# A graph network in two layers: TensorE's waits and semaphore raises gathered to one of each a chunk, and the sums of scores moved by one chunk

## The chip, the cores and the metric

The kernel runs on one core of one Trainium2 chip. A core has five engines that run their own instruction streams [...]: TensorE (PE in the profile, its weight loads PEld), VectorE (DVE), ScalarE (ACT), GpSimd (POOL) and SyncE (SP). An instruction that another one has to wait for raises its engine's semaphore when it ends; the one that waits does so until the semaphore has reached a given value. In this kernel SP issues the plain transfers between the chip's memory (HBM) and the core's own memory, and POOL issues the indirect ones, which gather or scatter single rows by a list of indices. The metric is the device time of one execution in microseconds, the median of the runs shown.

## What is computed

A graph of 10,000 nodes with 64 features each and 160,000 edges goes through two graph layers. The first is a softmax aggregation with four rounds, the second an attention without a division. Cut to what matters here:

```python
def genconv(x, src, dst, ea, ..., t):              # four rounds, l = 0..3
    m = relu(x[src] + ea) + EPS                    # one row for each edge
    logits = m * t
    mx = segment_max(logits, dst)
    e = exp(logits - mx[dst])
    denom = segment_sum(e, dst)
    agg = segment_sum(m * e / denom[dst], dst)
    h = (agg + x) @ W1 + b1
    return relu(layernorm(h)) @ W2 + b2

def attention(x, edge_attr, src, dst):             # once
    score = K[src] * Q[dst] / sqrt(8) * (edge_attr @ WE + bE)   # 8 heads of 8
    score = exp(clip(score.sum(over each head), -5, 5))
    return segment_sum(V[src] * score, dst)
```

The edges come sorted by dst, so every segment sum or maximum can be made as a scan along the edges with a mark where a new node begins.

## The kernel before

**Tiling.** The edge list is cut in two halves that lie on partitions 0 to 63 and 64 to 127, features down the partitions, edges along the free axis; the second half is walked backwards. A group is 128 edges of each half, a chunk four groups (512 columns). There are 625 groups and 158 chunks: 155 full ones, then two of two groups and one of one.

**A softmax layer** (`softmax_layer`, called four times, its layers are called 0 to 3 here). For chunk k, `front` has POOL gather eight blocks of 128 rows of the node table, one for each group and half (L738 through `gather`, L650), into a buffer `xg`, of which there are seven. TensorE then makes z: first the edge features times eencW (L740, one matmul over the whole chunk), then for each group the gathered rows, turned through the identity (L742), added on the same bank. The banks for z go round in five: z three times, then ept, then hist (`z_bank`; in layer 0 three of z alone). ScalarE takes z through a relu and the temperature (L745, L746) to `lg`, VectorE makes the running maximum (L752) and the difference (L754), ScalarE the exponentials (L757 to L767). `back`, for the chunk before, has VectorE make e*m (L780), two decaying scans (L782, L785), and two transposes (L811), and SP stores the result with four transfers (L815). SP also loads for each chunk, three chunks ahead, the marks (two transfers, L709) and the edge features (`load_ea`, L660, four buffers). Layer 0 has the edge features in rows: SP loads `er` (L667, L669), TensorE turns them (L678, L679), ScalarE copies them (L682) and SP stores them for the later layers (L683). Layer 0 also counts the nodes' edges as it goes: VectorE makes 0/1 matrices (`count`, L420, L423), TensorE multiplies them (`add_counts`, L429).

**Node layers.** Between two softmax layers `node_layer` gathers the sums of each node (POOL, `n_g`), runs the small matrices and writes the next table.

**The attention layer** (`attention_layer`). For each chunk SP loads the queries (L1045), the marks and the edge features; POOL gathers rows of keys and values (eight gathers again, into `kv`, a tile for two groups, seven tiles). `ahead` turns the queries on TensorE (L1055, bank oe), multiplies the edge features (L1058, bank hist), and VectorE spreads the queries by a scan (L1060) and multiplies (L1064, `eq`). `scores` turns keys (pk) and values (pv) on TensorE (L1084, three banks z in rotation), VectorE multiplies pk into eq (L1087), TensorE sums over each head (head_sum, L1089, bank dec). `weights` clips (VectorE, L1095) and takes the exponential (ScalarE, L1096). `back`, for the chunk before, multiplies pv by the weights (L1103), scans (L1105), transposes (L1116); SP stores with four transfers (L1120). At the end POOL gathers each node's row (`n_h`) and SP writes the output.

**Order.** The kernel is written in a language whose framework works out which instruction waits for which, from the buffers that they write and read, and sets the semaphores. An engine's instructions run in the order in which they stand in its stream; `InOrder` fixes that order to the order of the program text inside a layer. An instruction gets a semaphore raise when some wait counts on it: in the softmax layers before, all five matmuls of a chunk do, since each gather of chunk k+7 waits for the matmul that reads its own part of the buffer. Each matmul of L742 waits for its own two gathers.

Of the kernel before, what the change touches and what calls it, by code (L numbers as in the profile page):

```python
# [16 lines left out]
P = 128  # L17
# [9 lines left out]
def kernel(ctx: ExitStack, tc: tile.TileContext, a, out):  # L27
# [398 lines left out]

    def add_counts(ph, ol, oh, j0, j1):
        for k in range(j1 - j0):
            nc.tensor.matmul(ph, ol[:, k, :], oh[:, k, :], start=(j0 + k == 0),  # L429
                             stop=(j0 + k == R * KT - 1))  # L430

    def place_nodes(pool, cnt, tag):

# [213 lines left out]
    nc.vector.memset(zeros, 0.0)  # L647

    def gather(t, table, idx):
        nc.gpsimd.indirect_dma_start(out=t, out_offset=None, in_=table,  # L650
                                     in_offset=bass.IndirectOffsetOnAxis(ap=idx, axis=0))

    def span(k):
        g0, n = chunks[k]
# [2 lines left out]
    def load_ea(k):  # L657
        g0, n, cols = span(k)
        ea = edge.tile([P, CE], F32, name="ea", bufs=4)
        nc.sync.dma_start(ea[:, :n * G], eaT[:, cols])  # L660
        return ea

    def load_rows(k, ea_rows):
# [47 lines left out]

    V, S = nc.vector, nc.scalar

    def softmax_layer(l, ea_rows=None):

        prev = {}
        ph = ps("hist", [P, NT]) if ea_rows is not None else None
        per = 9
        if ph is not None:
# [12 lines left out]
        def front(k, marks, ea):  # L732
            g0, n, cols = span(k)
            m = n * G
            xg = edge.tile([P, CG, 2, D], F32, name="xg", bufs=7)
            for g in range(n):
                for s in range(2):
                    gather(xg[:, g, s, :], tables[l], index(g0 + g, s))  # L738
            z = z_bank(k)
            nc.tensor.matmul(z[:, :m], eencW, ea[:, :m], start=True, stop=False)  # L740
            for g in range(n):
                nc.tensor.matmul(z[:, g * G:(g + 1) * G], xg[:, g, :, :].rearrange("p s d -> p (s d)"),  # L742
                                 ident, start=False, stop=(g == n - 1))
            lg = ps("lg", [P, CE])
            S.activation(lg[:, :m], z[:, :m], AF.Relu)  # L745
# [80 lines left out]
        for k in range(NC):  # L826
            if k + lead < NC:
                got.append(fetch(k + lead))
            z, u, up, e = front(k, got[k][0], eas[k])
            if k + 2 < NC:  # L830
                eas.append(columns_of(k + 2))
            for c in counts:
                add_counts(*c)
            if counts and counts[-1][-1] == R * KT:
                rows_of_nodes(edge, ph)
            if held is not None:
                back(k - 1, *held)
            held = z, u, decay(k, up), e
            counts = history(k)
            order()  # L840
# [197 lines left out]
    def attention_layer():  # L1038

        prev = {}  # L1040

        def fetch(k):
            g0, n, cols = span(k)
            q = edge.tile([P, CG, 2, D], F32, name="q", tag="er", bufs=3)
            nc.sync.dma_start(  # L1045
                q[:, :n], qs[2 * g0 * G:2 * (g0 + n) * G, :].rearrange("(g p s) d -> p g s d", p=G, s=2))
            return load_marks(k, keeps_d), q, load_ea(k)

        def ahead(k, keep, q, ea):

# [7 lines left out]
            nc.tensor.matmul(pe[:, :m], WE, ea[:, :m], start=True, stop=True)  # L1058
            qh = edge.tile([P, CE], F32, name="qh", tag="u")
            V.tensor_tensor_scan(qh[:, :m], keep[:, :m], pq[:, :m], prev.get("q", zero1),  # L1060
                                 op0=OP.mult, op1=OP.add)
            prev["q"] = qh[:, m - 1:m]
            eq = edge.tile([P, CE], F32, name="eq", tag="sm")
            V.scalar_tensor_tensor(eq[:, :m], pe[:, :m], bE, qh[:, :m], op0=OP.add, op1=OP.mult)  # L1064
            return eq

        def fetch_kv(k):
            g0, n, cols = span(k)
            kvs = []
            for g in range(n):  # L1070
                if g % 2 == 0:
                    kvs.append(edge.tile([P, 2, 2, D2], F32, name="kv", tag="xg", bufs=7))
                for s in range(2):
                    gather(kvs[-1][:, g % 2, s, :], kv_table, index(g0 + g, s))
            return kvs

        def scores(k, kvs, eq):
            g0, n, cols = span(k)
            m = n * G
            pk = ps_a([P, CE])  # L1080
            pv = ps_a([P, CE])
            for pt, d0 in ((pk, 0), (pv, 1)):
                for g in range(n):
                    nc.tensor.matmul(pt[:, g * G:(g + 1) * G],  # L1084
                                     kvs[g // 2][:, g % 2].rearrange("p s d -> p (s d)")[:, d0::2],
                                     ident, start=True, stop=True)
            V.tensor_mul(eq[:, :m], pk[:, :m], eq[:, :m])  # L1087
# [123 lines left out]
```

## Time and profile before

| | |
|---|---|
| median of 3 runs | 10301.92 us (10288.25 to 10304.86) |
| the profiled execution's own time | 10286.74 us |
| its span in the trace | 10285.0 us |
| mean granted TensorE clock | 0.634 of full speed |
| gathers of softmax layer 0, from first start to last end | 159.5 to 1992.6 us |
| of layer 1 | 2223.1 to 3999.4 us |
| of layer 2 | 4217.1 to 5992.1 us |
| of layer 3 | 6210.4 to 7984.2 us |
| of the attention layer | 8338.0 to 10147.8 us |
| from a softmax layer's last gather to the next stage's first, layers 1 to 3 | 53.5 us |

The last six rows are read from the timeline of POOL. In a row of the costliest groups, the line and the engine come first, then the operation, what it writes and reads, how often, its busy time in us and the mean of one in ns, and after the second bar the idle time of the engine just before these instructions, with what ended most of it. "issue" is idle time for which the trace shows no wait; "remote" means that the trace doesn't tell who raised the semaphore that was waited for. In a timeline row, the start and the length in us come first, and the brackets hold the idle time before it. In a list of waits, a row gives the us in total, how many there were, and the longest. SP's rows have a q because they are its queue's own.

### The profile page before, as it was taken

What the parts mean: (1) busy time and instruction counts of PE and PEld (TensorE: products, weight loads), DVE (VectorE), ACT (ScalarE), POOL (GpSimd) and SP (SyncE); (2) the same over time, 40 slices, a digit from 0 to 9 for tenths busy, and PEclk for the clock granted to TensorE, in tenths of its full rate; (3) what the DMA queues carried; (4) which work ended last, traced back from release to release, by engine and by line L of the source; (5) the groups of instructions that cost most, each with busy time, mean ns of one, the idle gap of its engine ahead of it and who ended that gap; (6) DMA issues with size and microseconds to landing.
All of it is one profiled execution on the core that took longest, in us unless ns stands there. A gap on an engine that the chain in (4) does not pass through costs nothing. (4 is left out here: it accounts for less than half of the span.)

```text
span 10285.0 us, 67533 instructions
## 1 busy us (share of the span) xinstructions
PE 4024.4 (39%) x15722; PEld 2683.3 (26%) x15722; DVE 5480.7 (53%) x7537; ACT 2795.4 (27%) x4787; POOL 6369.3 (62%) x6736
## 2 busy tenths in 40 slices
PE   3444444452333333433333343333333444444442
PEld 1333333321222221222222222222222233333332
DVE  3767677625555554355555543555555445555553
ACT  1333333332333333333333332333333310000000
POOL 2666666556666665566666645666666456666665
PEclk8666666665655555655555565555556667777776
DMA  3555555654444444244444433444444235555553
GB/s 108 124 121 126 121 123 125 136 156 93 104 103 103 106 104 98 53 104 105 103 104 105 104 85 67 104 105 102 105 105 104 65 89 124 122 124 127 125 125 86
DMA packets 2467718, 1103.63 MB, mean 107 GB/s; under 512 B 2047265, under 2 KB 2239911, under 8 KB 2467088
## 3 DMA queue, kind: packets, MB, share of 16 engines
q1 hardware_dynamic: 2252120, 827.12, 34.1%
q0 software_dynamic: 215200, 272.11, 12.5%
q8 instruction: 140, 2.29, 0.1%
q14 instruction: 258, 2.11, 0.1%
HBM read 626.48 MB, written 471.91 MB: 107 GB/s over the span
## 5 line engine op out<-in xcount | busy, mean ns | idle before, releaser
L650 POOL DMA_INDIRECT xg<-table,idxA x2500 | 2364.9, 946 | 1939.4 <-remote 830.6
L650 POOL DMA_INDIRECT xg<-table,idxB x2500 | 2364.6, 946 | 763.1 <-issue 761.5
L752 DVE TENSOR_TENSOR_SCAN u<-lg,u,marks 128x512 f32<-128x512 f32 (+1 forms) x628 | 798.4, 1271 | 2712.9 <-ACT lg L746 1861.0
L740 PE MATMUL z<-ea,eencW 128*128 128x512 f32 (+1 forms) x892 | 872.0, 1079 | 2109.6 <-DMA marks<-ends_d 852.5
L742 PEld LDWEIGHTS z<-ident,xg 128*128 128x128 f32 x3512 | 802.6, 312 | 599.3 <-issue 572.4
L650 POOL DMA_INDIRECT kv<-kv_table,idxA x625 | 591.2, 946 | 434.6 <-remote 219.8
L742 PE MATMUL z<-ident,xg 128*128 128x128 f32 x3512 | 795.7, 396 | 157.6 <-DMA xg<-table,idxB 87.5
L740 PEld LDWEIGHTS z<-ea,eencW 128*128 128x128 f32 x892 | 226.7, 312 | 2191.5 <-issue 1907.2
L782 DVE TENSOR_TENSOR_SCAN se<-dec,se,e 128x512 f32<-128x512 f32 (+1 forms) x628 | 792.2, 1261 | 0.0
L785 DVE TENSOR_TENSOR_SCAN sm<-dec,sm,me 128x512 f32<-128x512 f32 (+1 forms) x628 | 782.2, 1246 | 0.0
L757 ACT ACTIVATE up<-lg 128x512 f32<-128x512 f32 (+1 forms) x632 | 374.4, 592 | 1360.2 <-issue 595.7
L650 POOL DMA_INDIRECT kv<-kv_table,idxB x625 | 591.2, 946 | 191.3 <-issue 189.5
L745 ACT ACTIVATE lg<-z 128x512 f32<-128x512 f32 (+1 forms) x446 | 249.1, 558 | 1539.0 <-remote 1180.4
L1089 PE MATMUL dec<-eq,head_sum 128*128 128x512 f32 (+2 forms) x316 | 236.2, 838 | 937.1 <-DVE eq L1087 897.9
L678 PE MATMUL ept<-ident,er 128*64 128x128 f32 x1250 | 270.2, 381 | 803.9 <-ACT ea L682 600.7
L1096 ACT ACTIVATE sc<-sc 128x512 f32<-128x512 f32 (+1 forms) x158 | 98.9, 626 | 1737.0 <-DVE sc L1095 788.8
L650 POOL DMA_INDIRECT n_g<-st,ends x316 | 302.0, 956 | 413.2 <-DMA marks<-ends_d 107.0
L767 ACT ACTIVATE dec<-up 128x512 f32<-128x512 f32 (+1 forms) x632 | 377.0, 596 | 657.0 <-issue 579.0
L746 ACT ACTIVATE lg<-lg,teps,tcol 128x512 f32<-128x512 f32 (+1 forms) x632 | 471.8, 746 | 21.1
L740 PE MATMUL ept<-ea,eencW 128*128 128x512 f32 x186 | 189.9, 1124 | 702.5 <-DMA ea<-eaT 303.9
L740 PE MATMUL hist<-ea,eencW 128*128 128x512 f32 x186 | 188.5, 1116 | 705.3 <-DMA marks<-ends_d 283.9
L1060 DVE TENSOR_TENSOR_SCAN qh<-marks,qh,oe 128x512 f32<-128x512 bf16 (+1 forms) x157 | 198.5, 1264 | 471.8 <-remote 417.4
(282 smaller groups left out, 8712.8 us busy)
## 6 DMA issues: line engine op xcount, KB each, us to landing
st<-so SPq DMA_DIRECT2D x2480, 128.0 KB
ea<-eaT SPq DMA_DIRECT2D x620, 256.0 KB
marks<-ends_d SPq DMA_DIRECT2D x1240, 64.0 KB
st<-so SPq DMA_DIRECT2D x652, 64.0 KB
xg<-table,idxA POOLq DMA_INDIRECT x2500
xg<-table,idxB POOLq DMA_INDIRECT x2500
qs<-zeros SPq DMA_DIRECT2D x156, 256.0 KB
er<-in_edge_attr_dram SPq DMA_DIRECT2D x310, 128.0 KB
```

Source lines behind the costliest of these rows:

```text
L650: nc.gpsimd.indirect_dma_start(out=t, out_offset=None, in_=table, in_offset=bass.IndirectOffsetOnAxis(ap=idx, axis=0))
L678: nc.tensor.matmul(pt[:D, g * G:(g + 1) * G], er[:, 0, g, :], ident, start=True, stop=True)
L740: nc.tensor.matmul(z[:, :m], eencW, ea[:, :m], start=True, stop=False)
L742: nc.tensor.matmul(z[:, g * G:(g + 1) * G], xg[:, g, :, :].rearrange("p s d -> p (s d)"), ident, start=False, stop=(g == n - 1))
L745: S.activation(lg[:, :m], z[:, :m], AF.Relu)
L746: S.activation(lg[:, :m], lg[:, :m], AF.Identity, bias=teps[:, l:l + 1], scale=tcol[:, l:l + 1])
L752: V.tensor_tensor_scan(u[:, 1:m + 1], lg[:, :m], marks[:, :m], last, op0=OP.max, op1=OP.add)
L757: S.activation(up[:, :m], lg[:, :m], AF.Relu)
L767: S.activation(dec[:, :m], up[:, :m], AF.Exp, scale=-1.0)
L782: V.tensor_tensor_scan(se[:, :m], dec[:, :m], e[:, :m], prev.get("e", zero1), op0=OP.mult, op1=OP.add)
L785: V.tensor_tensor_scan(sm[:, :m], dec[:, :m], me[:, :m], prev.get("m", zero1), op0=OP.mult, op1=OP.add)
L1089: nc.tensor.matmul(psc[:, :m], head_sum, eq[:, :m], start=True, stop=True)
```

## The change

Four things are done.

- `wait_for` adds a wait by hand: the first instruction waits until the second has ended. In the softmax layers the first matmul of a chunk (L740 before) now waits for all eight gathers; the matmuls behind it then need no wait of their own. Everything that reuses a buffer (the gathers of chunk k+7, the load of ea of chunk k+4) waits for the last matmul of the chunk, where before it waited for the one that read its part. So only that last matmul has to raise TensorE's semaphore, and it adds five at once.
- In layer 0 the same is done for the counts: VectorE's 0/1 matrices of a chunk wait for the last count of the chunk before, and the first count for the last matrix.
- In the attention layer the first of the sixteen-pass turns of keys and values waits for all gathers of the chunk, the gathers wait for the last turn of chunk k-3, the load of queries waits for the edge matmul of chunk k-3, the turn of the queries waits for the load of ea, the scan of the queries waits for the edge matmul, and VectorE's product with the keys waits for the last turn.
- `scores` ends with the product; head_sum's matmul moves into `weights`, which is called for chunk k-1 while chunk k is turned. `back` of chunk k-1 now stands after `ahead` of chunk k+1. `eq` gets a tag of its own with three buffers, and the keys' and values' banks are four (z, z, z, ept) in place of three.

```diff
     def add_counts(ph, ol, oh, j0, j1):
         for k in range(j1 - j0):
-            nc.tensor.matmul(ph, ol[:, k, :], oh[:, k, :], start=(j0 + k == 0),
-                             stop=(j0 + k == R * KT - 1))
+            ins = nc.tensor.matmul(ph, ol[:, k, :], oh[:, k, :], start=(j0 + k == 0),
+                                   stop=(j0 + k == R * KT - 1)).ins
+            if k == 0:
+                first = ins
+        return first, ins
...
+    def wait_for(ins, before):
+
+        if before is not None:
+            tc.add_manual_dep(
+                ins, before.name,
+                mybir.DependencyInfo(mybir.DependencyClass.Sync, mybir.DependencyReason.DATA),
+                reason="all of a chunk")
...
     def load_ea(k):
         g0, n, cols = span(k)
         ea = edge.tile([P, CE], F32, name="ea", bufs=4)
-        nc.sync.dma_start(ea[:, :n * G], eaT[:, cols])
+        loads[k] = nc.sync.dma_start(ea[:, :n * G], eaT[:, cols]).ins
+        wait_for(loads[k], done.get(k - 4))
         return ea
...
             xg = edge.tile([P, CG, 2, D], F32, name="xg", bufs=7)
+            z = z_bank(k)
+            got_all = []
             for g in range(n):
                 for s in range(2):
-                    gather(xg[:, g, s, :], tables[l], index(g0 + g, s))
-            z = z_bank(k)
-            nc.tensor.matmul(z[:, :m], eencW, ea[:, :m], start=True, stop=False)
+                    got_all.append(gather(xg[:, g, s, :], tables[l], index(g0 + g, s)))
+                    wait_for(got_all[-1], done.get(k - 7))
+            first = nc.tensor.matmul(z[:, :m], eencW, ea[:, :m], start=True, stop=False).ins
+            for ins in got_all:
+                wait_for(first, ins)
             for g in range(n):
-                nc.tensor.matmul(z[:, g * G:(g + 1) * G], xg[:, g, :, :].rearrange("p s d -> p (s d)"),
-                                 ident, start=False, stop=(g == n - 1))
+                done[k] = nc.tensor.matmul(
+                    z[:, g * G:(g + 1) * G], xg[:, g, :, :].rearrange("p s d -> p (s d)"),
+                    ident, start=False, stop=(g == n - 1)).ins
...
             j0, j1 = min(k * per, R * KT), min((k + 1) * per, R * KT)
-            return [count(edge, ph, j, min(j + 5, j1), numbers) for j in range(j0, j1, 5)]
+            seen = len(nc.cur_bb.bb.instructions)
+            made = [count(edge, ph, j, min(j + 5, j1), numbers) for j in range(j0, j1, 5)]
+            for ins in nc.cur_bb.bb.instructions[seen:]:
+                wait_for(ins, prev.get("counted"))
+                prev["numbers"] = ins
+            return made
...
-            for c in counts:
-                add_counts(*c)
+            for i, c in enumerate(counts):
+                first, prev["counted"] = add_counts(*c)
+                if i == 0:
+                    wait_for(first, prev["numbers"])
...
             for g in range(n):
-                nc.tensor.matmul(pq[:, g * G:(g + 1) * G], q[:, g, :, :].rearrange("p s d -> p (s d)"),
-                                 ident, start=True, stop=True)
+                ins = nc.tensor.matmul(pq[:, g * G:(g + 1) * G], q[:, g, :, :].rearrange("p s d -> p (s d)"),
+                                       ident, start=True, stop=True).ins
+                if g == 0:
+                    wait_for(ins, loads[k])
             pe = ps("hist", [P, CE])
-            nc.tensor.matmul(pe[:, :m], WE, ea[:, :m], start=True, stop=True)
+            done[k] = nc.tensor.matmul(pe[:, :m], WE, ea[:, :m], start=True, stop=True).ins
             qh = edge.tile([P, CE], F32, name="qh", tag="u")
-            V.tensor_tensor_scan(qh[:, :m], keep[:, :m], pq[:, :m], prev.get("q", zero1),
-                                 op0=OP.mult, op1=OP.add)
+            wait_for(V.tensor_tensor_scan(qh[:, :m], keep[:, :m], pq[:, :m], prev.get("q", zero1),
+                                          op0=OP.mult, op1=OP.add).ins, done[k])
             prev["q"] = qh[:, m - 1:m]
-            eq = edge.tile([P, CE], F32, name="eq", tag="sm")
+            eq = edge.tile([P, CE], F32, name="eq", tag="eq", bufs=3)
...
+        def bank():
+
+            prev["bank"] = prev.get("bank", -1) + 1
+            return ps("ept", [P, CE]) if prev["bank"] % 4 == 3 else ps_a([P, CE])
+
         def scores(k, kvs, eq):
             g0, n, cols = span(k)
             m = n * G
-            pk = ps_a([P, CE])
-            pv = ps_a([P, CE])
+            kvs, got_all = kvs
+            pk, pv = bank(), bank()
+            first = None
             for pt, d0 in ((pk, 0), (pv, 1)):
                 for g in range(n):
-                    nc.tensor.matmul(pt[:, g * G:(g + 1) * G],
-                                     kvs[g // 2][:, g % 2].rearrange("p s d -> p (s d)")[:, d0::2],
-                                     ident, start=True, stop=True)
-            V.tensor_mul(eq[:, :m], pk[:, :m], eq[:, :m])
+                    turned_kv[k] = nc.tensor.matmul(
+                        pt[:, g * G:(g + 1) * G],
+                        kvs[g // 2][:, g % 2].rearrange("p s d -> p (s d)")[:, d0::2],
+                        ident, start=True, stop=True).ins
+                    if first is None:
+                        first = turned_kv[k]
+            for ins in got_all:
+                wait_for(first, ins)
+            wait_for(V.tensor_mul(eq[:, :m], pk[:, :m], eq[:, :m]).ins, turned_kv[k])
+            return pv
+
+        def weights(k, eq):
+            m = span(k)[1] * G
             psc = ps("dec", [P, CE])
             nc.tensor.matmul(psc[:, :m], head_sum, eq[:, :m], start=True, stop=True)
-            return pv, psc
-
-        def weights(k, psc):
-            m = span(k)[1] * G
             sc = edge.tile([P, CE], F32, name="sc", tag="e")
...
-        for k in range(NC):
-            kvs = fetch_kv(k)
-            if k + 2 < NC:
-                got.append(fetch(k + 2))
-            pv, psc = scores(k, kvs, made)
+        for k in range(NC + 1):
+            pv = None
+            if k < NC:
+                kvs = fetch_kv(k)
+                if k + 2 < NC:
+                    got.append(fetch(k + 2))
+                pv, eq = scores(k, kvs, made), made
             if held is not None:
-                back(k - 1, *held)
-            held = got[k][0], pv, weights(k, psc)
+                sc = weights(k - 1, held[1])
             if k + 1 < NC:
                 made = ahead(k + 1, *got[k + 1])
+            if held is not None:
+                back(k - 1, got[k - 1][0], held[0], sc)
+            held = pv, eq
             order()
-        back(NC - 1, *held)
         order()
```

`fetch` of the attention layer wraps its load of the queries in `wait_for(..., done.get(k - 3))`, and `fetch_kv` returns its gathers beside the tiles and has each of them wait for `turned_kv.get(k - 3)`.

More of the change, by code (lines that the diff above doesn't have):

```diff
@@ L649, in gather @@
     def gather(t, table, idx):
-        nc.gpsimd.indirect_dma_start(out=t, out_offset=None, in_=table,
-                                     in_offset=bass.IndirectOffsetOnAxis(ap=idx, axis=0))
+        return nc.gpsimd.indirect_dma_start(out=t, out_offset=None, in_=table,
+                                            in_offset=bass.IndirectOffsetOnAxis(ap=idx, axis=0)).ins
+    def wait_for(ins, before):
[4 more added lines that the diff above has]
+                reason="all of a chunk")
     def span(k):
@@ L712 @@
     V, S = nc.vector, nc.scalar
+    done, loads = {}, {}
     def softmax_layer(l, ea_rows=None):
         prev = {}
+        done.clear()
         ph = ps("hist", [P, NT]) if ea_rows is not None else None
@@ L1040, in attention_layer @@
         prev = {}
+        done.clear()
         def fetch(k):
@@ L1044, in fetch @@
             q = edge.tile([P, CG, 2, D], F32, name="q", tag="er", bufs=3)
-            nc.sync.dma_start(
-                q[:, :n], qs[2 * g0 * G:2 * (g0 + n) * G, :].rearrange("(g p s) d -> p g s d", p=G, s=2))
+            wait_for(nc.sync.dma_start(
+                q[:, :n], qs[2 * g0 * G:2 * (g0 + n) * G, :].rearrange("(g p s) d -> p g s d", p=G, s=2)).ins,
+                done.get(k - 3))
             return load_marks(k, keeps_d), q, load_ea(k)
+        turned_kv = {}
         def ahead(k, keep, q, ea):
@@ L1068, in fetch_kv @@
             g0, n, cols = span(k)
-            kvs = []
+            kvs, got_all = [], []
             for g in range(n):
@@ L1073, in fetch_kv @@
                 for s in range(2):
-                    gather(kvs[-1][:, g % 2, s, :], kv_table, index(g0 + g, s))
-            return kvs
+                    ins = gather(kvs[-1][:, g % 2, s, :], kv_table, index(g0 + g, s))
+                    got_all.append(ins)
+                    wait_for(ins, turned_kv.get(k - 3))
+            return kvs, got_all
+        def bank():
+            prev["bank"] = prev.get("bank", -1) + 1
+            return ps("ept", [P, CE]) if prev["bank"] % 4 == 3 else ps_a([P, CE])
         def scores(k, kvs, eq):
```

## The prediction

> **What bounds the kernel now.** I read the page's busy shares and costliest groups first, then POOL's waits in one softmax layer, then the timeline around one of POOL's long waits, then the same in the attention layer. All times are of the one profiled execution.
>
> ```profile
> PE 4024.4 (39%) x15722; PEld 2683.3 (26%) x15722; DVE 5480.7 (53%) x7537; ACT 2795.4 (27%) x4787; POOL 6369.3 (62%) x6736
> ...
> L650 POOL DMA_INDIRECT xg<-table,idxA x2500 | 2364.9, 946 | 1939.4 <-remote 830.6
> L650 POOL DMA_INDIRECT xg<-table,idxB x2500 | 2364.6, 946 | 763.1 <-issue 761.5
> ...
> L745 ACT ACTIVATE lg<-z 128x512 f32<-128x512 f32 (+1 forms) x446 | 249.1, 558 | 1539.0 <-remote 1180.4
> ```
>
> No engine is full, POOL is nearest. It does little but gathers: 1250 a layer, five layers. The waits of POOL between 4217 and 5993 us, which is layer 2's gathers from first to last:
>
> ```profile
> POOL xg L650 <- issue: 363.5, 1191, 0.6
> POOL xg L650 <- remote: 206.1, 25, 8.8
> ```
>
> Two kinds of idle time: 363.5 / 1191 = 0.305 us before nearly every gather, so one gather costs 0.946 + 0.305 = 1.251 us wherever nothing holds it (10.0 us for a chunk's eight), and 25 long waits of about 8.2 us. 1250 x 1.251 = 1564, and 1564 + 206 = 1770: the layer's gathers take 1775.0 us (first start to last end). So a softmax layer is POOL's gathers plus these 25 waits. The semaphore they wait for is TensorE's: the first gather of chunk k refills the buffer of chunk k-7. The timeline shows what TensorE was doing:
>
> ```profile
> 3017.15 2.05 PE L740 MATMUL z<-ea,eencW 128*128 128x512 f32 x2 [3.40 <-issue]
> 3018.99 1.78 PE L742 MATMUL z<-ident,xg 128*128 128x128 f32 x8
> 3029.02 2.04 PE L740 MATMUL z<-ea,eencW 128*128 128x512 f32 x2 [8.26 <-issue]
> ...
> 3041.15 0.58 ACT L745 ACTIVATE lg<-z 128x512 f32<-128x512 f32 x1 [11.34 <-remote]
> 3041.74 1.19 PE L740 MATMUL ept<-ea,eencW 128*128 128x512 f32 x1 [8.96 <-DMA ea<-eaT]
> ...
> 3054.15 0.95 POOL L650 DMA_INDIRECT xg<-table,idxB  x1 [0.30 <-issue]
> 3064.05 0.95 POOL L650 DMA_INDIRECT xg<-table,idxA  x1 [8.95 <-remote]
> ...
> 3002.74 2.35 SPq L815 DMA_DIRECT2D st<-so  x4
> 3057.34 4.26 SPq L815 DMA_DIRECT2D st<-so  x4
> ```
>
> Banks go z, z, z, ept, hist, and ACT at 3015.92 read hist and at 3022.83 the first z; so its read at 3041.15 is of the chunk that TensorE began at 3017.15 and ended at 3020.77. ACT was idle for 11.34 us and got word 20.4 us after the last matmul. TensorE was not busy: it stood still for 8 to 9 us between chunks. What is late is the raise of its semaphore. Each matmul here carries one (L740 and four of L742, five a chunk), and chunks come 11.9 and 12.7 us apart: 12.7 / 5 = 2.5 us a raise if the raises pace them. The bound from above is 20.4 / 5 = 4.1 us. SP's four stores take 4.26 us to issue in this stretch, and 2.35 us at 3002.74, when gathers ran as densely but TensorE had no matmul for 9 us. So the crawl needs TensorE's raises beside the gathers. The attention layer shows it more plainly:
>
> ```profile
> 9209.73 1.02 PE L1058 MATMUL hist<-ea,WE 128*128 128x512 f32 x2
> 9221.25 1.28 DVE L1060 TENSOR_TENSOR_SCAN qh<-marks,qh,oe 128x512 f32<-128x512 bf16 x1 [10.19 <-remote]
> 9227.03 0.69 DVE L1087 TENSOR_TENSOR eq<-z,eq 128x512 f32<-128x512 f32 x1 [1.50 <-remote]
> 9227.32 0.95 POOL L650 DMA_INDIRECT kv<-kv_table,idxA  x1 [3.74 <-remote]
> ```
>
> The scan needs only matmuls that were over by 9209.9 (L1055 before this L1058), and starts 11.3 us later; the gather needs matmuls of 9212.6 and starts 14.7 us later.
>
> [...]
>
> **The change, part by part.** Counted in the two built programs over all layers that run, TensorE's raises go from 5461 to 1979.
>
> *Softmax layers 1 to 3.* Five raises a chunk become one, on the last matmul, adding 5 at once. At 2.5 us a raise TensorE's semaphore then needs 2.5 us of a 10.0 us chunk, so nothing queues; POOL's 25 waits go. POOL's gathers stay: same 1250, same 1.251 us. Late next is POOL itself: VectorE and ACT repeat in 6.91 us a chunk when fed (scans at 4005.24 and 4012.16). New waits: the first matmul waits for eight gathers, so L740 (2.05 us) no longer runs while gathers land. Behind it on TensorE is only the rest of the chunk; POOL's slack is seven buffers, 70 us, and five banks give ACT 50 us: nothing, except once at each layer's end, about 2 us. The load of ea on SP waits for the chunk's last matmul instead of L740, 4 us later; the stores behind it need VectorE's work on the same chunk, later still: nothing. Per layer: gathers 1775 to 1564 + 3 for odd waits = 1567 (1776.3 + 1775.0 + 1773.8 - 3 x 1567 = 624 us). At the end POOL now idles 53.5 us before the next stage's gathers, because VectorE is six chunks behind; kept up, it is about two short chunks and a store behind, 23 us by 6.91 us a chunk: 30 us a layer, 90 us.
>
> *Layer 0.* Raises 7.75 a chunk to about 2.9 (z 1, L679 1, counts 0.9). 1833.1 us of gathers, floor 1564. VectorE's loop is 8.3 us at best here (counting included), TensorE turns rows behind the now later chunk, so I keep 36 us of waits: 1600, 233 us less, and 30 us at the end.
>
> *Attention.* Raises 9 a chunk to 3.5. Floor 1564 of 1809.8. Here the change also moves work: head_sum's matmul, the clip and the exponential act on chunk k-1, and the product with the values, its scan, transpose and four stores come on VectorE after the query scan and eq of k+1 instead of before. SP's and POOL's order past it stays (fetches, then stores). The queries' scan now waits for the L1058 matmul too (1.02 to 2.1 us). That closes a loop: L1058's raise R, scan 1.26, eq 0.75, product 0.68, value half of the next chunk's transposes 1.0 to 1.7, head_sum 1.1 to 2.1, queries and edges 2.0 to 3.6: 6.8 to 10.1 us plus R, by TensorE's clock (0.72 on average here, so about 8.3). With R under 1.5 us it hides beneath POOL's 10.0. Bounds: 1564 with all hidden; 1810 if nothing is gained. I take 1625, 185 us less. Kv buffers now come back per chunk, three ahead instead of three and a half: 30 us of slack against about 10, nothing.
>
> Sum: 624 + 90 + 233 + 30 + 185 = 1162. Profiled execution 10286.7 (span 10285.0 and 1.7 around it) - 1162 = 9125; the median of the runs is 15 higher, so 9140.
>
> **Rivals.**
> *Part of it stays.* Single raises still meet the crawl when head_sum, edges and values follow each other, or layer 0 stays as it is: for it, 3.5 x 2.5 = 8.75 us a chunk in attention is near 10. Against it, most attention chunks before run undelayed with nine. Layer 0 and attention unchanged: 9140 + 233 + 30 + 185 = 9590.
> *The raises are a symptom.* SP's slow issue (about 1.4 us for each of its nine steps, 12.6 us a chunk) paces the stretch and raises queue behind it; then it stays and the time is about 10,280. For it: TensorE's waits end on loads of ea. Against it: SP is fast at 3002.74 amid gathers.
> *Slower: the attention loop.* If a raise keeps its 6 us delay behind others there (two raises at 2.5 us ahead, and its own), the loop is 8.3 + 6 = 14.3 us, 158 x 14.3 = 2259, 449 more; with softmax unchanged 10,750. It decides once R passes 10.0 - 8.3 + 1.5 = 3.2 us and the softmax layers gain nothing.
>
> **How the numbers follow.** Forecast 0.70, part 0.14, symptom 0.08 (half within 0.2%, the rest split), slower loop 0.08. All floors at once (1564 five times is 1148 less, 150 off the ends) give 8989 + 15, hence a low end of 9000; upwards the range takes in the partial case and a little of what lies past it, 9650. Faster by over 0.2% (21 us, about what a measurement of this kernel can tell from no change): 0.70 + 0.14 + 0.02 = 0.86, within 0.04, slower 0.10.
>
> **What would show it.** Right: POOL's remote waits in layers 1 to 3 near zero, gathers of a layer in some 1567 us, ACT's L745 soon after the chunk's last matmul, SP's four stores near 2.3 us throughout, under 30 us from a layer's last gather to the next stage's. Wrong: the 8 us waits are still there, or the scan of the queries waits on the edge matmul for microseconds in most chunks.

## The result and the profile after

The changed kernel is slower by a quarter of a per cent: median 10,326.64 us of 13 runs beside 10,298.57 us, ratio 1.0026 (95% interval 1.0017 to 1.0034). In two later sets of runs in which the kernel before took 10,234 and 10,235 us, the ratio was 1.0049 (1.0016 to 1.0081) and 1.0028 (1.0010 to 1.0046). Nine of the changed kernel's 21 runs in these two sets, at 10,458 to 10,552 us, are left out of the ratios, while none of the 37 runs of the kernel before was over 10,247 us, and why is not known. I had forecast 9,140 us.

The page of the changed kernel, in the rows that answer to those shown of before (the `gather` helper is now L653, ACT's first read of a chunk L765):

```profile
PE 4176.1 (41%) x15722; PEld 2787.0 (27%) x15722; DVE 5478.0 (53%) x7537; ACT 2793.6 (27%) x4787; POOL 6354.3 (62%) x6736
...
L653 POOL DMA_INDIRECT xg<-table,idxA x2500 | 2358.8, 944 | 1947.6 <-remote 820.5
L653 POOL DMA_INDIRECT xg<-table,idxB x2500 | 2359.0, 944 | 762.6 <-issue 760.5
...
L765 ACT ACTIVATE lg<-z 128x512 f32<-128x512 f32 (+1 forms) x446 | 249.0, 558 | 1603.4 <-remote 1235.9
```

POOL's idle time "remote" was 830.6 us and is 820.5; ACT's was 1180.4 and is 1235.9. Nothing that the change was expected to end has ended. POOL's waits in layer 2's gathers (4213 to 5988 us; total, times, longest):

```profile
POOL xg L653 <- issue: 405.7, 1203, 39.1
POOL xg L653 <- remote: 222.2, 26, 9.9
```

Before had 25 such waits "remote" and 206.1 us; here are 26, the longest 9.9 us. (The 405.7 contains one wait of 39.1 us for the layer's start.) From first to last gather, in us:

| gathers of | layer 0 | layer 1 | layer 2 | layer 3 | attention | span |
|---|---|---|---|---|---|---|
| before | 1833.1 | 1776.3 | 1775.0 | 1773.8 | 1809.8 | 10285.0 |
| after | 1829.3 | 1776.3 | 1774.6 | 1773.8 | 1829.2 | 10306.7 |

Layers 1 to 3 are the same to half a microsecond, layer 0 gained 3.8 us, and the attention layer lost 19.4. The rest of the span's 21.7 us lies outside these gathers, most of it at the ends of layers 1 to 3: POOL was idle there for 53.5 us before the next stage's gathers and is idle for 55.4. The timeline of the changed kernel at the place where before was read:

```profile
3001.04 2.04 PE L757 MATMUL z<-ea,eencW 128*128 128x512 f32 x2 [8.36 <-DMA marks<-ends_d]
...
3003.77 4.96 SPq L840 DMA_DIRECT2D st<-so  x4
...
3012.34 0.58 ACT L765 ACTIVATE lg<-hist 128x512 f32<-128x512 f32 x1 [11.06 <-remote]
...
3013.69 2.04 PE L757 MATMUL z<-ea,eencW 128*128 128x512 f32 x2 [8.90 <-DMA ea<-eaT]
...
3025.85 2.05 PE L757 MATMUL z<-ea,eencW 128*128 128x512 f32 x2 [8.56 <-DMA marks<-ends_d]
...
3034.93 0.58 ACT L765 ACTIVATE lg<-z 128x512 f32<-128x512 f32 x1 [15.58 <-remote]
3035.16 0.94 POOL L653 DMA_INDIRECT xg<-table,idxA  x1 [8.70 <-remote]
```

The bank z that TensorE began at 3001.04 was full at 3004.79 and is read at 3034.93, 30 us later, though its one raise has no other raise of the same chunk ahead of it. SP's four stores still take 5 us. Three raises, of three chunks, are recorded at 3034.90, 3035.01 and 3035.80: they had been held back together, and were let go within 0.9 us. So it is not a matter of 2.5 us each.

In the attention layer the queries' scan (now L1093) still waits: in 127 of 158 chunks it starts over 2 us after the end of the edge matmul, 4.8 us on average, and VectorE's "remote" idle time before it has gone from 417.4 to 595.4 us. Here it comes 6.8 us after that end:

```profile
9117.76 1.02 PE L1091 MATMUL hist<-ea,WE 128*128 128x512 f32 x2
...
9125.59 1.28 DVE L1093 TENSOR_TENSOR_SCAN qh<-marks,qh,oe 128x512 f32<-128x512 bf16 x1 [7.83 <-remote]
```

One measure is used below. *Lateness* is the time from the end of a chunk's last transposing matmul to ACT's first read of its bank, both from the trace. Over the full chunks of layers 1 to 3 it has a mean of 20.2 us before and 20.2 us after, with 9.3 to 9.4 at the 10th and 30.2 at the 90th percentile. The largest, 70 to 72 us, come in the first ten chunks of a layer. *The crawl* is the name used below for this state, in which raises are 20 us late and the 1250 gathers of each of layers 1 to 3 take 1,765 to 1,776 us in these two kernels.

### The profile page after: what moved, and what is told of

Its sections match the earlier page's. It is cut to its first block, busy times and chain, and to the rows that moved or that the text cites. A ratio compares the mean times of both kernels' runs of the same rounds, so it can differ in the third digit from the quotient of the medians.

```text
span 10306.7 us, 67069 instructions
## 1 busy us (share of the span) xinstructions
PE 4176.1 (41%) x15722; PEld 2787.0 (27%) x15722; DVE 5478.0 (53%) x7537; ACT 2793.6 (27%) x4787; POOL 6354.3 (62%) x6736
## 5 line engine op out<-in xcount | busy, mean ns | idle before, releaser
L653 POOL DMA_INDIRECT xg<-table,idxA x2500 | 2358.8, 944 | 1947.6 <-remote 820.5
L653 POOL DMA_INDIRECT xg<-table,idxB x2500 | 2359.0, 944 | 762.6 <-issue 760.5
L653 POOL DMA_INDIRECT kv<-kv_table,idxA x625 | 589.6, 943 | 457.5 <-issue 166.2
L761 PE MATMUL z<-ident,xg 128*128 128x128 f32 x3512 | 770.3, 390 | 71.6 <-issue 64.2
L653 POOL DMA_INDIRECT kv<-kv_table,idxB x625 | 589.8, 944 | 190.8 <-issue 189.2
L765 ACT ACTIVATE lg<-z 128x512 f32<-128x512 f32 (+1 forms) x446 | 249.0, 558 | 1603.4 <-remote 1235.9
L653 POOL DMA_INDIRECT n_g<-st,ends x316 | 301.4, 954 | 420.1 <-DMA marks<-ends_d 110.8
L1093 DVE TENSOR_TENSOR_SCAN qh<-marks,qh,oe 128x512 f32<-128x512 bf16 (+1 forms) x157 | 198.3, 1263 | 659.3 <-remote 595.4
L774 DVE TENSOR_TENSOR lg<-lg,u 128x512 f32<-128x512 f32 (+1 forms) x632 | 438.2, 693 | 21.9
```

What stands on the lines that cost most here:

```text
L653: return nc.gpsimd.indirect_dma_start(out=t, out_offset=None, in_=table, in_offset=bass.IndirectOffsetOnAxis(ap=idx, axis=0)).ins
L761: done[k] = nc.tensor.matmul(z[:, g * G:(g + 1) * G], xg[:, g, :, :].rearrange("p s d -> p (s d)"), ident, start=False, stop=(g == n - 1)).ins
L1093: wait_for(V.tensor_tensor_scan(qh[:, :m], keep[:, :m], pq[:, :m], prev.get("q", zero1), op0=OP.mult, op1=OP.add).ins, done[k])
```

## The experiments

Two theories stood after the result: that each *unit* of a raise costs its 2.5 us (the one raise adds 5), and that the raises are a symptom of SP's slow queue. A third came out of the second set of runs. (A unit is one step that a raise adds to the semaphore's value.) Each set ran on one chip, together with runs of the kernel before.

**First set: the crawl is not always there.** Four kernels: each half of the change alone, five tiny matmuls more in a chunk, and SP's loads moved to ACT's queue.

```diff
# softmax_only, attention_only: the other half as before
# more_raises, ahead of each chunk's first matmul:
+            for _ in range(5):
+                nc.tensor.matmul(z[:, :4], eencW, ea[:, :4], start=True, stop=True)
# loads_act, in load_ea and load_marks:
-nc.sync.dma_start(
+nc.scalar.dma_start(
```

> The softmax layers as changed (first matmul waits for all gathers, one raise a chunk), the attention layer as before. Theory 'raises are a symptom of SP's queue': layers 1 to 3 keep 1774 to 1776 us of gathers, attention goes back to 1810, the time is that of before, 10,299 +- 10. Theory 'each unit of a raise costs': the same here, so this run does not divide the two; it divides the place of the loss: if the loss is in attention, this is at 10,299; if it came from the softmax part, at 10,326.

> The softmax layers as before, the attention layer as changed. If the loss lies in the attention layer: gathers there 1829, the time 10,320 to 10,328. If not: 10,299.

> The changed kernel with five tiny matmuls (128x4, overwritten after) put ahead of every softmax chunk, so that one raise a chunk adds 10 in place of 5. Theory 'each unit costs 2.5 us': the crawl goes at 25 us a chunk in place of 12.5, a layer takes well over 2,500 us, the whole 13,000 or more. Theory 'a symptom of SP's queue': layers 1 to 3 at 1775 +- 10, whole 10,327 to 10,345.

> The changed kernel with the loads of marks and ea on ACT's DMA queue in place of SP's, so that SP issues four DMAs a softmax chunk and ACT three. Theory 'SP's issue at 1.4 us a step paces the crawl': SP needs under 7 us a chunk, the long waits of POOL go, layers 1 to 3 near 1570, the whole near 9,550. Theory 'the landing of HW DMAs paces it [...]': the same seven in a chunk, no gain, layers 1775 or more, as ACT now stands behind late raises too; whole 10,300 to 10,700. Theory 'each unit of a raise costs': no gain either.

The unchanged kernel before took 8,847.6 us here (8,844.3 to 8,850.0, 33 runs), not 10,299. softmax_only took 8,859.3 (ratio 1.0013, 1.0007 to 1.0020), attention_only 8,853.5 (1.0005, 0.9997 to 1.0014), more_raises 8,868.6 and loads_act 8,904.9. In all of them the gathers of layers 1 to 3 took 1,560 us, lateness was 0.04 us, and POOL bound every layer. The timeline of attention_only, whose softmax layers are those of before:

```profile
4302.16 2.26 SPq L826 DMA_DIRECT2D st<-so  x4
...
4303.82 0.77 PE L753 MATMUL ept<-ident,xg 128*128 128x128 f32 x2 [1.73 <-DMA xg<-table,idxB]
...
4304.38 1.92 PE L751 MATMUL hist<-ea,eencW 128*128 128x512 f32 x2
...
4304.62 0.58 ACT L756 ACTIVATE lg<-ept 128x512 f32<-128x512 f32 x1 [3.04 <-PE ept L753]
```

ACT reads 0.03 us after the last matmul's end at 4304.59, with five raises a chunk and gathers running. The premise of my forecast, that five raises beside gathers make the crawl, is therefore wrong: here were both, and no crawl. The two theories could not be told apart where there was nothing to explain. The set does tell what the change costs by itself (below).

**Second set: SP's queue.** This set met the crawl again: before took 10,233.6 us. The kernel `pairs` is the kernel before, with marks loaded and sums stored for two chunks at once:

```diff
+            half["t"] = edge.tile([P, 2 * CE], BF, name="marks", bufs=3)
...
+            if k % 2 == 0:
+                prev["so"] = edge.tile([P, 2 * CE // 32, 2, 32], F32, name="so2", bufs=2), g0
...
+            if k % 2 == 1 or k == NC - 1:
...
                 for q in range(4):
                     nc.sync.dma_start(rows_out[q // 2, q % 2],
```

> The kernel before, unchanged, for a trace beside the others. In the first four runs it took 8,847.6 us where it had taken 10,299 when the change was measured, so the crawl is no property of the program alone. If the crawl is absent: gathers of layers 1 to 3 in 1560 us each, no wait of POOL over 2 us inside a layer, TensorE's raises at ACT within 0.3 us of the chunk's last matmul, SP's DMAs landing in 2 to 3 us. If it is present: 1774 to 1776 us a layer, as in the first trace, and the whole near 10,290.

> The changed kernel, unchanged. With the crawl absent, the two parts add: 8,847.6 + 11.7 (softmax part alone) + 5.9 (attention part alone) = 8,865 +- 4, ratio 1.002; if the parts share a cause, less. With the crawl present: 10,327 beside 10,299, ratio 1.0026.

> The kernel before with marks loaded and sums stored for two chunks at once, so that a softmax chunk costs SP 4 DMAs in place of 7; TensorE's raises untouched at five a chunk. With the crawl present: theory 'SP's queue paces it' has 4 x 1.4 to 1.8 = 5.6 to 7.2 us a chunk, under the 10.0 of the gathers, so the crawl cannot hold: 1565 to 1580 us a layer, the whole 9,300 to 9,600; theory 'the raises pace it' has no gain: 10,299 or above. With the crawl absent: POOL bounds every layer and nothing is gained, 8,848 to 8,870 (later stores at the layers' ends cost a few us).

before_again took 10,232.4 us with 1,765.9, 1,765.1 and 1,766.4 us of gathers in layers 1 to 3. after_again has the first of the two later ratios above. pairs took 10,235.2 us (ratio 1.0001, 0.9993 to 1.0010), with 1,763.2, 1,765.9 and 1,767.7. Four DMAs a chunk in place of seven did nothing, so SP's queue doesn't pace the crawl. Its timeline says more:

```profile
3015.30 0.69 SPq L660 DMA_DIRECT2D ea<-eaT  x1
...
3023.59 2.07 PE L748 MATMUL hist<-ea,eencW 128*128 128x512 f32 x2 [5.31 <-DMA xg<-table,idxB]
3025.46 0.42 PE L750 MATMUL hist<-ident,xg 128*128 128x128 f32 x1
3026.52 0.37 PE L750 MATMUL hist<-ident,xg 128*128 128x128 f32 x1 [0.64 <-issue]
3028.64 0.37 PE L750 MATMUL hist<-ident,xg 128*128 128x128 f32 x1 [1.74 <-issue]
3030.72 0.37 PE L750 MATMUL hist<-ident,xg 128*128 128x128 f32 x1 [1.72 <-issue]
3033.52 0.37 PE L750 MATMUL hist<-ident,xg 128*128 128x128 f32 x1 [2.42 <-issue]
...
3036.34 0.58 ACT L753 ACTIVATE lg<-z 128x512 f32<-128x512 f32 x1 [9.80 <-PE hist L750]
3036.58 0.94 POOL L650 DMA_INDIRECT xg<-table,idxA  x1 [7.13 <-PE hist L750]
```

SP issues nothing between 3015.99 and 3036 us, and TensorE is held all the same: matmuls for which the trace shows no wait start 2 to 3 us apart. It ends at 3036.3, some 7 us after POOL's last gather, with raises recorded 42 to 43 ns apart. This looks as if something were full and drained once POOL rests. What POOL does then became the third theory: *each gather loads something with about 1.41 us of work; gathers come every 1.25 us; TensorE's raises and SP's steps wait behind it*. It fits a number that was in the first profile: 1775 / 1250 = 1.42 us a gather in the softmax layers, and 1810 / 1250 = 1.45 in attention, with nine raises a chunk there and five here.

**Third set: units, pace and rows.** Before took 10,238.5 us: the crawl was there. Three ladders, one step a layer:

```diff
# raise_ladder, on the changed kernel:
+            for _ in range(5 if l == 1 else 0):
+                nc.tensor.matmul(z[:, :4], eencW, ea[:, :4], start=True, stop=True)
...
-            for g in range(n):
+            for g in range(n - 1 if l == 3 else 0, n):
# pad_ladder, on the kernel before, after each gather:
+                    for _ in range(l):
+                        nc.gpsimd.memset(pad, 0.0)
# rows_ladder, on the kernel before, R_ = (128, 128, 64, 96)[l]:
-                    gather(xg[:, g, s, :], tables[l], index(g0 + g, s))
+                    gather(xg[:R_, g, s, :], tables[l], index(g0 + g, s)[:R_])
```

> The changed kernel with another number of units in TensorE's one raise a chunk in each layer: layer 1 has five tiny matmuls more (10 units), layer 2 is unchanged (5), layer 3 leaves out three of the four transposes of the gathered rows (2 units; the sums of layer 3 lack those rows). Where the crawl is present: theory 'each unit costs 2.5 us' says gathers of layer 1 in 158 x 25 = 3,950 us, layer 2 in 1,767, layer 3 in 1,565. Theory 'the gathers themselves fill something at about 1.41 us each, and the raises queue behind it' says 1,766 +- 10 in all three, as what counts is 1250 gathers. Where the crawl is absent: 1,560 in layers 2 and 3 under both; layer 1 1,560 under the second, and this run then divides nothing.

> The kernel before with l short writes of 128x1 on POOL after each gather of layer l, so that gathers start about 1.25, 1.4, 1.55 and 1.7 us apart in layers 0 to 3. Where the crawl is present: theory 'gathers fill something at about 1.41 us each' says the long waits of POOL go in layers 2 and 3 and nearly so in layer 1, TensorE's raises come within 0.5 us there, SP's waiting instructions take 17 ns and not 700, and layer 1 takes no longer than unpadded, 1,750 to 1,790; layers 2 and 3 are then 1250 periods long. Theory 'raises or SP's queue pace a chunk at 12.5 us' says layers 1 and 2 (11.2 and 12.4 us of gathers a chunk) keep raises that are late by 10 us and more, and layer 1 is still 1,775. Where the crawl is absent: each layer is 1250 periods long, no waits.

> The kernel before with gathers of fewer rows at the same number of gathers: 128 rows in layers 0 and 1, 64 in layer 2, 96 in layer 3 (the other rows are left out of the sums). Where the crawl is present: if what the gathers fill is counted in rows (descriptors), layer 2 is free of it and takes POOL's own time, 1,250 x 1.25 or less; layer 3 too (96/128 x 1.41 = 1.06 us). If it is counted in gathers, or if raises or SP pace the chunk, layers 2 and 3 stay at 1,766, or long waits stay in any case. Where the crawl is absent this run only prices a gather by its rows.

| gathers of layer, us | 0 | 1 | 2 | 3 |
|---|---|---|---|---|
| raise_ladder: 5, 10, 5, 2 units in layers 0 to 3 (counts apart) | 1814.8 | 1779.8 | 1766.8 | 1758.7 |
| pad_ladder: 0, 1, 2, 3 writes | 1831.5 | 1782.9 | 1805.9 | 1993.0 |
| its lateness, mean | 7.1 | 25.1 | 0.04 | 0.04 |
| rows_ladder: 128, 128, 64, 96 rows | 1814.4 | 1765.7 | 1768.9 | 1764.7 |

The cost by units, which asked for 3,950 us with ten and 1,565 with two, falls. Five units more than in layer 2 cost 13.0 us over 158 chunks and three fewer save 8.1: as an estimate from this one run, 16 to 17 ns a unit. Layer 3 of raise_ladder even has raises that come at once (mean lateness 0.27 us) and takes 1,758.7 us all the same. Its gathers in the list of groups (busy time, mean ns of one, idle time before):

```profile
L653 POOL DMA_INDIRECT xg<-table,idxA x625 | 611.1, 978 | 381.1 <-issue 362.6 <-DMA xg<-table,idxA 11.5 <-PE hist L763 4.4
L653 POOL DMA_INDIRECT xg<-table,idxB x625 | 608.8, 974 | 197.1 <-issue 197.1
```

Where POOL does not wait for a late raise it is slowed itself: 978 ns a gather, not 944, and more idle time that no semaphore ends.

pad_ladder is the clearest. One short write fits into the 0.30 us that POOL is idle before a gather in the kernel before (two of them take 0.27 us in pad_ladder's layer 2), so that in layer 1 the median start is still 1.25 us after the one before, and raises are late. Two writes bring the starts to 1.36 us, with a pause at each chunk 1.445 on average (1805.9 / 1250), and the crawl is gone:

```profile
5001.80 0.77 PE L745 MATMUL z<-ident,xg 128*128 128x128 f32 x2 [2.82 <-DMA xg<-table,idxB]
...
5002.60 0.58 ACT L748 ACTIVATE lg<-z 128x512 f32<-128x512 f32 x1 [5.85 <-PE z L745]
...
5010.20 2.12 SPq L818 DMA_DIRECT2D st<-so  x4
...
5012.87 0.76 PE L745 MATMUL z<-ident,xg 128*128 128x128 f32 x2 [2.48 <-DMA xg<-table,idxB]
...
5013.68 0.58 ACT L748 ACTIVATE lg<-z 128x512 f32<-128x512 f32 x1 [4.07 <-issue]
```

ACT reads 0.03 to 0.05 us after the last matmul ends; the four stores take 2.1 us. TensorE's raises, five a chunk, and SP's seven DMAs are those of before. What differs is the pace of the gathers, and the writes that make it. I had expected waits to be nearly gone in layer 1 as well; they have only moved. POOL waits on a semaphore or for no visible reason before its short writes, 186 us in 316 waits, where the first trace had long waits before gathers, 222 us in 28; of those, 28 us in 20 are left. Layer 1 takes 1782.9 us all the same.

rows_ladder: 64 rows and 96 rows load as much as 128 (1768.9 and 1764.7 us beside 1765.7). The load does not go by rows.

**Fourth and fifth sets: very few rows, and gathers that wait for nothing.** The fourth set met no crawl (before 8,856.7 us), so few_rows and free_run only gave POOL's own pace: 1,428, 1,443 and 1,473 us for layers of 16, 8 and 4 rows a gather; 1,560 with the stores left out or the transposes left out. ladder3 asked again in the fifth set (before 10,234.9 us). Its edit joins the two:

```diff
+            R_ = (128, 16, 4, 128)[l]
...
-            nc.tensor.matmul(z[:, :m], eencW, ea[:, :m], start=True, stop=False)
-            for g in range(n):
+            nc.tensor.matmul(z[:, :m], eencW, ea[:, :m], start=True, stop=l == 3)
+            for g in range(n if l < 3 else 0):
```

> The kernel before with gathers of very few rows, as many gathers as before: 128 rows in layer 0, 16, 8 and 4 in layers 1, 2 and 3 (the other rows are left out of the sums). Where the crawl is present: theory 'a fixed load of about 1.41 us for each gather, whatever its size' says gathers of layers 1 to 3 in 1,766 +- 15 us each, still with long waits of POOL. [...] Where the crawl is absent: POOL's own pace in all layers.

> The kernel before; layer 1 leaves out the four stores of a chunk (the sums are those of layer 0), layer 2 is unchanged, layer 3 leaves out the transposes of the gathered rows (its sums lack them), so that no gather waits for TensorE. Where the crawl is present: theory 'gathers load something at 1.41 us each' says layer 1 is no shorter (1,766 +- 15) though SP issues three DMAs a chunk in place of seven; in layer 3 POOL is not held and gathers take 1,560 to 1,580 us, while SP and TensorE still crawl and end late by about 1250 x (1.41 - 1.25) = 200 us. Theory 'SP's queue paces the crawl' says layer 1 at 1,565. If POOL itself is held by what is full, layer 3 stays at 1,766.

> The kernel before with 128 rows a gather in layer 0, 16 in layer 1, 4 in layer 2 (other rows left out of the sums), and in layer 3 whole gathers whose transposes are left out, so that no gather waits for TensorE. Without the crawl the same layers took 1,560, 1,428, 1,474 (4 rows) and 1,560 us. Where the crawl is present: theory 'a fixed load of 1.41 us a gather' says 1,766 +- 15 in layers 1 and 2[...]. Layer 3: 1,560 to 1,580 if POOL is held only through TensorE's raises, 1,766 if it is held itself.

Layers 1 and 2 took 1,767.3 and 1,767.2 us, where 16 and 4 rows had taken 1,428 and 1,473 without the crawl. The load is the same for 4 rows as for 128. Layer 3, where no gather waits for TensorE, took 1,729.8 us, neither 1,560 nor 1,766. The timeline of ladder3's POOL, near the start of layer 3 and far into it:

```profile
6191.03 0.94 POOL L650 DMA_INDIRECT xg<-table,idxB  x1 [0.30 <-issue]
6192.28 0.94 POOL L650 DMA_INDIRECT xg<-table,idxA  x1 [0.30 <-issue]
...
7001.79 1.10 POOL L650 DMA_INDIRECT xg<-table,idxA  x1 [0.30 <-issue]
7003.19 1.12 POOL L650 DMA_INDIRECT xg<-table,idxB  x1 [0.30 <-issue]
7004.62 1.10 POOL L650 DMA_INDIRECT xg<-table,idxA  x1 [0.30 <-issue]
```

The first 150 gathers start 1.248 us apart. From about the 200th on they start 1.403 to 1.408 us apart, in every stretch of 50 to the layer's end, each gather itself longer by 0.16 us. So POOL itself is held from then on, at 1.405 us a gather, as if what it fills were full. What was stored by then is, as an estimate, some 175 x (1.405 - 1.249) = 27 us of work. That is near the lateness of 30.2 us at the 90th percentile, but it does not account for the sixth to ninth chunks of a layer, whose reads are 49 to 72 us late in the first trace.

**What the change costs by itself.** The halves were run twice, both times without the crawl, and the whole change three times, each time with it.

> The same kernel as in the first four runs (softmax layers as changed, attention as before), beside a before in the crawl this time. Earlier it cost 11.7 us without the crawl. If the loss with the crawl is also at the layers' ends: 5 to 12 us over before. If the softmax part is what makes the changed kernel's times spread (10,228 to 10,543 in nine runs): some runs 200 to 300 us above the others.

> The same kernel as in the first four runs (softmax layers as before, attention as changed). Earlier 5.9 us without the crawl. From the two first traces the attention layer's gathers took 19.4 us longer with the change: 10 to 25 us over before. If the attention part is what makes the changed kernel's times spread: some runs 200 to 300 us above the others.

> The changed kernel, unchanged. Without the crawl: before + 12 (softmax part) + 5 (attention part) = before + 17 +- 4 us, ratio 1.002, close together. With the crawl: ratio 1.0026 to 1.005, with some runs 200 to 300 us above the others.

softmax_part: 8,868.9 beside 8,856.7, ratio 1.0014 (1.0008 to 1.0021). attention_part: 8,861.8, ratio 1.0006 (0.9998 to 1.0014), an interval that includes no change at all. Between a layer's last gather and the next stage's first, softmax_part has 2.9, 3.0, 3.0 and 3.0 us more than attention_part at its four ends, nearly all of its 12.2 us. This fits the part of the change by which TensorE's first matmul, which used to run ahead of the last gathers, now follows them. After the last gather of the attention layer the span goes on for 123.7 us in attention_part and 119.0 in softmax_part, 4.7 us of the 5 that the attention part costs. With the crawl, after_third's attention gathers took 1,796.5 us beside 1,789.8 of before_again, 6.7 us more, as in after_again; in the first two traces it was 19.4. Which of the attention layer's edits makes this was not settled, and the halves were not run where the crawl was present.

## Why the prediction was wrong

*The step that failed* is "12.7 / 5 = 2.5 us a raise if the raises pace them", and with it "the crawl needs TensorE's raises beside the gathers". The raises do not pace the chunk. Where many are let go one behind the other they are 43 ns apart (median of 1,430 pairs under 70 ns apart in the first trace), and a unit more or less moved a chunk by 16 to 17 ns, by the estimate above. With 10, 5 or 2 units a chunk a layer took 1779.8, 1766.8 and 1758.7 us. The 12.7 us was also the longer of two periods shown: over the layer eight gathers take 8 x 1775.0 / 1250 = 11.4 us, near 8 x 1.405 = 11.2. The runs fit raises that wait behind a load that comes with the gathers. Dividing one period by the one count at hand gave a plausible price; that attention, with nine raises, needs about as much for a gather was not asked of it.

*Softmax layers 1 to 3, 624 us less:* nothing, 0.4 us in all three. *Layer 0, 233 less:* 3.8. *Attention, 185 less:* 19.4 more. The queries' scan waits for microseconds in most chunks, as the prediction's own sign of being wrong had it. *Layer ends, 90 and 30 less:* the gain there rested on the same premise and did not come. *"Except once at each layer's end, about 2 us"* held: 1.9 us with the crawl, 2.9 to 3.0 without.

*"Late next is POOL itself", some 1,567 us a layer,* is right where the crawl is absent: 1,560. But the kernel before does that too, and needs no fewer raises for it.

*The rival "the raises are a symptom"* named the time well (10,280) and half of the reason. Its cause, SP's issue of 1.4 us a step, fell with pairs. My reason against it was that SP is fast at 3002.74 amid gathers. There one of POOL's long waits had ended 7.4 us before. In layers 1 to 3 of the first trace the four stores take 2.2 to 3.6 us in all 147 chunks in which they start within 15 us of the end of one of POOL's long waits, and 3.5 to 5.7 us in the 282 later ones, so SP's speed goes with POOL's rest. TensorE's idle 9 us, to which I gave the credit, is not needed for it: in pad_ladder SP is fast beside gathers and raises alike. *The slower attention loop* had the right sign, not the size: scans come 11.6 us apart in both first traces (11.57 and 11.65). Its threshold has a slip: a loop of 8.3 us plus R passes 10.0 once R is over 1.7 us; the 1.5 added to make it 3.2 was allowed for nowhere.

The first trace held the measure against the price: raises let go together are 43 ns apart there, and 2.5 us is 58 times as much. I should have taken that gap as a sign that something other than raises was measured.

*Open:* what a gather fills. It is not counted in rows: layer 2 took 1,767.2 us with 4 rows a gather (ladder3) and 1,765.1 with 128 (before_again). What it consists of, and why it needs 1.405 us a gather, was not shown by any run.

Every chunk in every run has eight gathers, so a load that comes once a chunk, with VectorE's or ACT's work say, would look the same in these totals. Two things speak for the gathers: POOL's own gathers are stretched in ladder3, and raises, SP's DMAs and rows could be changed without moving a layer by more than some 15 us. That is an argument, not a proof. The runs on record also come with traced spans, so that a part played by the tracing itself is not excluded.

Open too is why the crawl is present in some sets and absent in others. The record names the chips of the five later sets: 0 and 14 without the crawl, 10, 4 and again 10 with it. That fits a property of the chip, but no chip is known to have given both, and no run separates a chip from its surroundings.

## What to carry to other kernels

A late signal is not yet a slow signal: before pricing an event by dividing a period by its count, divide the same stretch by every other count, and take the one that gives the same figure in stages that differ in the rest. Of the counts tried here, raises, SP's DMAs, rows and gathers, only the gathers did. Here gathers that start every 1.25 us where only 1.405 us could be kept up (ladder3, layer 3) showed as delay at other engines, in bursts, and it ended when POOL rested; padding the suspected source, and seeing whether the delays vanish (mean lateness 25.1 us with one write, 0.04 with two), was a cheap test. And a premise from one trace about a chip's behaviour needs a second set of runs before time is promised on it.

## What the runs showed of the hardware that was not expected

- The same program took 10,299, 10,234, 10,238 and 10,235 us in four sets of runs and 8,848 and 8,857 us in two, each with little spread. In the four, none of the layers given above took under 1,729.8 us for its 1250 gathers, and ladder3's layer 3, where no gather waits for TensorE, went from 1.248 us between starts to 1.403 to 1.408 after some 200 gathers; in the two, 1.248 to 1.250 us was kept up, all layers through.
- With the crawl, TensorE's raises arrive 20.2 us late on average, 30.2 at the 90th percentile (lateness in layers 1 to 3 of both first traces). Of SP's waiting instructions in layer 2 of the first trace, 157 of 296 take 650 to 750 ns; in layer 3 of pad_ladder all 307 take 17. ACT's raises come at once even then: in the changed kernel's first trace one is recorded at 2943.96, and VectorE's scan starts on it at 2943.99. All 474 such scans of its layers 1 to 3 start 32 to 34 ns after the end of ACT's work on the chunk.
- An indirect gather cost POOL nearly the same for 4 to 128 rows: without the crawl, start to start 1.249 us for 128 rows (attention_only), 1.14 for 16, 1.15 for 8 and 1.18 for 4 (few_rows).
